# Layer 2 of a four-layer kernel computed in layer 1's order of columns

## The chip, the cores and the metric

The kernel runs on one core of one Trainium2 chip. The metric is the device time of one execution in microseconds (us). A core has TensorE (PE, with its weight loads as PEld), VectorE (DVE), ScalarE (ACT), GpSimd (POOL) and SyncE (SP), each with an instruction stream of its own that runs in order; they wait for each other through semaphores, and DMA queues move data beside them.

## The reference

The input x has the shape (4, 8, 512, 512): 4 images t of 8 channels, rows and columns. Four layers each add to x a layer applied to x normalised in groups (`_gn`: 4 groups of 2 channels, mean and variance over the group's channels, rows and columns).

```python
x = x + _L0_conv_ref(_gn(x), ...)   # spiking attention: four products, heads, a scan over t
x = x + _L1_conv_ref(_gn(x), w)     # 13x13 convolution of each channel by itself, reflected borders
x = x + _L2_conv_ref(_gn(x), weight, bias)
x = x + _L3_conv_ref(_gn(x), weight, bias)

def _L2_conv_ref(x, weight, bias):
    sx = MAX_Q / jnp.max(jnp.abs(x))
    sw = MAX_Q / jnp.max(jnp.abs(weight))
    qx = _quantize(x, sx)           # clip(round(v * scale), -127, 127)
    qw = _quantize(weight, sw)
    out_i32 = conv 3x3 of qx and qw, 8 to 8 channels, zeros as padding
    return out_i32 / (sx * sw) + bias

def _L3_conv_ref(input, weight, bias):
    return conv 3x3 of input and weight, 8 to 8 channels, zeros as padding, + bias
```

The change is in layer 2 and touches neither layer 0 nor layer 1.

## The kernel before, in words

Layers 0 and 1 come first and take the first 2511 us. Layer 1 works on columns in four phases: column 4v + g of a row is held at place 128 g + v (g from 0 to 3, v from 0 to 127; PH is 4, NV is 128, D is 512). It writes its result to DRAM (x2d) in this order, called phase order here. Layer 3 and the output need the columns in their own order.

Layers 2 and 3 share one loop (`layers23`, from L1009). A tile has 128 partitions, which hold two windows of 8 rows by 8 channels (6 rows of results each), and 512 columns. 43 tiles make an image; two tiles are a pair, the last pair of an image has one tile of 64 partitions, so an image has 22 pairs and the loop 88 pairs in all, one a step. In step n:

- `load` (L1053) issues pair n + 5's load of x from x2d on SP's queue, into one of 6 buffers.
- `normalise` (L1077) works on pair n + 2. GpSimd copies each tile of x into a tile u and turns phase order into the own order on the way (L1083: reads 128 columns of one phase in a row, writes every fourth place). ScalarE computes y, u scaled and shifted by the group's statistics and by sx (L1088).
- `quantise` (L1095) works on pair n + 1: VectorE rounds y to whole numbers by adding and subtracting a large constant and writes bf16 into xq (L1100), one of three buffers with two columns of zeros on both sides.
- `layer2` (L1109) works on pair n. For each tile TensorE does three bf16 matmuls, one for each horizontal offset dx of the 3x3 kernel (L1118); the vertical offsets and channels are in the weights. VectorE multiplies the product by inv, adds u and writes x3 (L1125, scalar_tensor_tensor), and for some tiles also sums the result on the way (`accum_out`). x3 is a ring in SBUF that holds layer 3's input. The statistics for layer 3's norm come from ScalarE's sum of squares (L1131) for those tiles, which are all full ones for t = 0 and every second one later, and from VectorE's bn_stats (L1136) for the others.
- `halos` (L1140, issued at L1275) copies the rows that neighbouring windows share, by DMA inside x3; SP issues these copies in the first 22 steps and GpSimd after that.
- `layer3` (L1205) works on the pair 25 steps back. GpSimd writes the two edge columns (L1213), TensorE does 24 fp32 matmuls of 64 by 64 (L1220), ScalarE adds the constant (L1229), SP issues the output DMA (L1236).

When an image's last pair has gone through layer 2, `norm3` (L1165) brings its statistics together in small steps: VectorE L1171 to L1182 and L187 to L196, two small TensorE products (L180, gps from gsum), GpSimd's power (L197), and then VectorE makes layer 3's weights band_t (L1189), a value scaled (L1193) and, after a small product ps_const (L1198), the constant (L1202). Layer 3 of that image can't start before these.

The order of the work on each engine is decided when the kernel is built, by a scheduler that is steered by `issue_after`: normalise and quantise are issued behind the last instructions of layer 2, and layer 2 behind them and behind layer 3. So an instruction that waits holds up all that stands behind it on its engine.

Of the kernel before, what the change touches and what calls it, by code (L numbers as in the profile page):

```python
# [31 lines left out]
F32 = mybir.dt.float32  # L35
BF16 = mybir.dt.bfloat16
F16 = mybir.dt.float16
F32R = mybir.dt.float32r
AF = mybir.ActivationFunctionType
ALU = mybir.AluOpType  # L40
# [3 lines left out]
P = 128  # L44
T, B, N, D, H = 4, 8, 512, 512, 8
# [7 lines left out]
ROUND = 12582912.0  # L53
# [3 lines left out]
PH, NV = 4, D // 4  # L57
# [10 lines left out]
N_PAIRS = (W_ALL + 3) // 4  # L68
# [12 lines left out]
def windows(k):  # L81

    p, j = divmod(k, 2)
    every = [(a, 4 * p + 2 * j + (a ^ j)) for a in range(2)]
    return [(a, q) for a, q in every if q < W_ALL]
# [43 lines left out]
def network(ctx: ExitStack, tc: tile.TileContext, i: dict, out: bass.AP):  # L129
    nc = tc.nc  # L130
# [100 lines left out]
    def pool(name, bufs=1, **where):  # L231
        return tc.tile_pool(name=name, bufs=bufs, reuse_waits="tile", **where)
# [4 lines left out]
    r2 = late.tile([P, T, G], F32, name="r2")  # L237
    most = late.tile([P, G], F32, name="most")
    early = {
        "x": ctx.enter_context(pool("x2", 6, side="right")),  # L240
        "u": ctx.enter_context(pool("u2", 4, side="right")),
        "y": ctx.enter_context(pool("y2", 2, side="right")),
        "o": ctx.enter_context(pool("o3", 10, side="right")),
    }
# [16 lines left out]
    with ExitStack() as s:  # L261
        layers23(
            s, tc, x2d, out, ident, ind, mask2, avg_same, group_steps, m2, r2, most, w23, early, pool
        )
# [628 lines left out]
def weights23(tc, i, pool, scratch, ps_1, ident):  # L893


    nc = tc.nc
# [5 lines left out]
    w = {}  # L902
# [65 lines left out]
    ps = ps_1.tile([P, 2, n_taps], F32, tag="misc", name="ps_outer2")  # L968
# [21 lines left out]
            )  # L990


    w["xq"] = [pool.tile([P, 2, D + 4], BF16, name=f"xq_{j}") for j in range(3)]
    for xq in w["xq"]:
        nc.gpsimd.memset(xq, 0.0)
    w["st3"] = [pool.tile([P, W2_N, 6], F32, name=f"st3_{j}") for j in range(2)]
# [12 lines left out]
def layers23(  # L1009
    s, tc, x2d, out, ident, ind, mask2, avg_same, group_steps, m2, r2, most, w, early, pool  # L1010
):
    nc = tc.nc
# [9 lines left out]
    ps = ps_1.tile([1, P], F32, tag="misc", name="ps_most")  # L1022
# [7 lines left out]
    ps = ps_1.tile([P, 1], F32, tag="misc", name="ps_top")  # L1030
# [6 lines left out]
    for mine, src in ((w["m"], m2), (w["r"], r2)):  # L1037
        own = wpool.tile([P, T, G], F32, tag="own", name="own")
# [7 lines left out]

    x3 = s.enter_context(pool("x3")).tile([P, 2 * RING, D + 2], F32, name="x3")

    def tiles(p):
        return [k for k in (2 * p, 2 * p + 1) if k < W2_N]  # L1050

    def slot(t, p):
        return 2 * ((t * N_PAIRS + p) % RING)  # L1053

    ahead, ready = {}, {}
# [17 lines left out]
    def tiles_apart(t, p, n):  # L1073

        return [slice(j, j + 1) for j in range(n)] if (t, p) == (0, 0) else [slice(0, n)]

    def normalise(t, p):  # L1077
        n, n_p = len(tiles(p)), HALF * len(windows(tiles(p)[-1]))
        x = ahead.pop((t, p))[:n_p, :n, :]
        u = early["u"].tile([P, 2, D], F32, tag="u", name="u2")  # L1080
        y = early["y"].tile([P, 2, D], F32, tag="y", name="y2")
        for j in range(n):
            nc.gpsimd.tensor_copy(  # L1083
                u[:n_p, j, :].rearrange("p (v g) -> p v g", g=PH),
                x[:, j, :].rearrange("p (g v) -> p v g", g=PH),
            )
        for j in tiles_apart(t, p, n):
            op = nc.scalar.activation(  # L1088
                y[:n_p, j, :], u[:n_p, j, :], AF.Identity, bias=w["mr"][:n_p, t : t + 1],
                scale=w["r"][:n_p, t : t + 1],  # L1090
            )
        ready[t, p] = u, y[:n_p, :n, :]
        return op.ins

    def quantise(t, p):  # L1095
        u, y = ready[t, p]
        n_p, n, _ = y.shape
        xq = w["xq"][(t * N_PAIRS + p) % 3]
        for j in tiles_apart(t, p, n):
            op = nc.vector.tensor_scalar(  # L1100
                xq[:n_p, j, 2 : D + 2], y[:, j, :], ROUND, ROUND, op0=ALU.add, op1=ALU.subtract
            )
        ready[t, p] = u, xq
        return op.ins

    def by_sums(t):
        return range(0 if t == 0 else 1, W2_N - 1, 1 if t == 0 else 2)

    def layer2(t, p):  # L1109
        ks = tiles(p)  # L1110
        n_p = HALF * len(windows(ks[-1]))
        u, xq = ready.pop((t, p))
        s0 = slot(t, p)
        st3 = w["st3"][t % 2]
        for j, k in enumerate(ks):
            ps = ps_2.tile([P, D], F32, tag="conv2", name="ps_conv2")
            for dx in range(3):
                mm = nc.tensor.matmul(  # L1118
                    ps[:n_p, :], lhsT=w["band2"][:n_p, j, dx, :n_p],
                    rhs=xq[:n_p, j, dx + 1 : dx + 1 + D], start=dx == 0, stop=dx == 2,  # L1120
                )
            own = x3[:n_p, s0 + j, 1 : D + 1]
            sums = w["sums"][t % 2][:, :, k : k + 1]
            summed = k in by_sums(t)
            done["DVE"] = nc.vector.scalar_tensor_tensor(  # L1125
                own, ps[:n_p, :], w["inv"][:n_p], u[:n_p, j, :], op0=ALU.mult, op1=ALU.add,
                accum_out=sums[:, 0, :] if summed else None,
            ).ins
            if summed:
                square = wpool.tile([P, D], BF16, tag="square", name="square")  # L1130
                done["ACT"] = nc.scalar.activation(  # L1131
                    square, own, AF.Square, bias=w["m"][:, t : t + 1], scale=-1.0,
                    accum_out=sums[:, 1, :],
                ).ins
            else:
                done["DVE"] = nc.vector.bn_stats(st3[:n_p, k, :], own).ins  # L1136
        return mm.ins
# [68 lines left out]
    def layer3(t, p, zero, band, const):  # L1206


        ks = tiles(p)
        s0 = slot(t, p)  # L1210
        n_p = HALF * len(windows(ks[-1]))
# [36 lines left out]
    for n in range(n_all + N_PAIRS + LAG):  # L1248
        if n < n_all:
            for m in range(6) if n == 0 else [n + 5]:  # L1250
                if m < n_all:
                    load(*divmod(m, N_PAIRS))


            with ExitStack() as order:
                for op in done.values():
                    order.enter_context(tc.issue_after(op))
                for m in range(3) if n == 0 else [n + 2]:
                    if m < n_all:
                        first = normalise(*divmod(m, N_PAIRS))  # L1260
                for m in range(2) if n == 0 else [n + 1]:
                    if m < n_all:
                        then = quantise(*divmod(m, N_PAIRS))
            with ExitStack() as order:
                for op in (first, then, *behind):
                    order.enter_context(tc.issue_after(op))
                did = layer2(*divmod(n, N_PAIRS))
        next(norm, None)
        if n_chunk < n <= n_all + 3 and n % n_chunk == 3:
            t, p = divmod(n - 3 - n_chunk, N_PAIRS)  # L1270
# [5 lines left out]
        if n >= N_PAIRS + LAG:  # L1276
            t, p = divmod(n - N_PAIRS - LAG, N_PAIRS)
# [41 lines left out]
```

## Time and profile before

| | us |
|---|---|
| median of 3 runs | 2932.97 (2931.45 to 2935.19) |
| the profiled execution | 2934.12 |
| its span in the profile | 2932.3 |
| layers 0 and 1, until about | 2511 |
| layer 2 of t = 0 alone | 2511 to about 2565 |
| first matmul of layer 3 (L1220) | 2588.2 |
| layers 2 and 3 together, until about | 2860 |
| layer 3 alone, until about | 2924 |

TensorE is busy for 2826.4 us of the span, VectorE for 2210.8, GpSimd for 1036.6, ScalarE for 551.0; the mean granted TensorE clock is 0.989 of full speed.

In the profile, a group of instructions is named by its line in the kernel, engine and operation, then what it writes and reads with the shapes, the count, the busy time and the mean duration of one in ns, and after the bar the time that the engine was idle just before it and what ended most of that. In a timeline, each line has the start in us, the duration in us, the instruction and in brackets the idle time before it with its cause; neighbouring instructions of one kind are drawn together (x2, x6).

### The profile page before, as it was taken

The page shows a single profiled execution, that of the slowest core. Times are in us where ns is not written, and L with a number is a line of the kernel's source. Part 1 is how long each engine was busy: PE and PEld are TensorE (multiplying, and loading weights), DVE is VectorE, ACT ScalarE, POOL GpSimd, SP SyncE. Part 2 cuts the span into 40 slices and gives each one's busy share as a digit, 9 for nine tenths or more (in the row PEclk, how much of TensorE's full clock was granted, in tenths as well). Part 3 has the DMA queues.
Part 4 walks back from the last instruction along what each step waited for, and adds up shares of the span by engine and source line. Part 5 has one row for each costly group of instructions (what it writes and reads, how often), then busy time and mean ns, then how long its engine had stood idle before and what let it go on. Part 6 is the DMA issues. An engine that isn't in the chain of part 4 may idle for free. (4 is left out here: it accounts for less than half of the span.)

```text
span 2932.3 us, 36617 instructions
## 1 busy us (share of the span) xinstructions
PE 2826.4 (96%) x12865; PEld 1302.0 (44%) x12865; DVE 2210.8 (75%) x3916; ACT 551.0 (19%) x860; POOL 1036.6 (35%) x1924
## 2 busy tenths in 40 slices
PE   6899999999999999999999999999999999589999
PEld 3454555554555544455455555455333333223334
DVE  7897788688779778868877886886655556887870
ACT  1300010011010001001000000110111111766664
POOL 3342233343234323323422433332211112676650
PEclk9899999999999999999999999999999999999999
DMA  7333322223222223222222122113878779698865
GB/s 182 100 81 80 73 59 66 72 71 78 64 66 66 73 76 70 59 66 66 73 66 51 45 59 51 52 44 87 224 194 222 207 200 242 145 212 214 221 171 147
DMA packets 323895, 322.10 MB, mean 110 GB/s; under 512 B 21431, under 2 KB 237183, under 8 KB 323599
## 3 DMA queue, kind: packets, MB, share of 16 engines
q1 hardware_dynamic: 261872, 237.39, 33.4%
q0 software_dynamic: 19776, 56.14, 6.0%
q10 hardware_dynamic: 42063, 26.23, 3.2%
q8 instruction: 101, 1.65, 0.3%
q14 instruction: 83, 0.68, 0.1%
HBM read 210.57 MB, written 103.60 MB: 107 GB/s over the span
## 5 line engine op out<-in xcount | busy, mean ns | idle before, releaser
L499 PE MATMUL ps_in<-w_v,xn 128*128 128x512 f32 x1024 | 459.2, 598 | 3.0 <-DVE xn L480 3.0
L499 PE MATMUL ps_in<-w_kq,xn 128*128 128x512 f32 x1024 | 450.1, 592 | 0.0
L815 PE MATMUL ps_conv<-x,bt 112*64 112x512 f32 x2048 | 445.0, 592 | 0.8 <-DVE v_p L467 0.8
L499 PE MATMUL ps_in<-xn,w_kq 128*128 128x512 f32 x1024 | 444.6, 592 | 0.0
L535 PE MATMUL ps_b<-toep,vtok 128*64 128x512 bf16 x3072 | 368.9, 384 | 1.0 <-DVE v_o L550 1.0
L475 POOL TENSOR_TENSOR h_v<-h_v,c_v 128x512 f32<-128x512 f32 x96 | 122.0, 1271 | 683.9 <-DVE h_v L474 658.2
L450 ACT ACTIVATE h_q<-v_q,c_half 128x512 f32<-128x512 f32 x96 | 69.2, 721 | 1473.6 <-DVE v_q L446 950.4
L584 POOL COPY x1s<-x1s 128x2 f32<-128x2 f32 (+1 forms) x1024 | 227.7, 277 | 272.3 <-DVE x1s L573 272.3
L562 PE MATMUL ps_out<-wp,so 128*128 128x512 f32 x1024 | 308.9, 444 | 0.0
L499 PEld LDWEIGHTS ps_in<-xn,w_kq 128*128 128x128 f32 x1024 | 194.3, 190 | 233.0 <-issue 223.2
L499 PEld LDWEIGHTS ps_in<-w_kq,xn 128*128 128x128 f32 x1024 | 194.2, 190 | 219.9 <-issue 204.7
L499 PEld LDWEIGHTS ps_in<-w_v,xn 128*128 128x128 f32 x1024 | 190.9, 191 | 218.4 <-issue 210.1
L815 PEld LDWEIGHTS ps_conv<-x,bt 112*64 112x64 f32 x2048 | 144.9, 135 | 290.2 <-issue 288.1
L1220 PE MATMUL ps_conv<-x,band_t 64*64 64x512 f32 x2040 | 251.4, 609 | 3.1 <-DVE band_t L1189 3.1
L535 PEld LDWEIGHTS <-vtok 128*64 128x64 bf16 x3072 | 176.0, 111 | 155.5 <-issue 7.0
L1083 POOL COPY u<-x 128x512 f32<-128x512 f32 (+1 forms) x172 | 211.7, 1266 | 91.8 <-issue 48.2
L562 PEld LDWEIGHTS ps_out<-wp,so 128*128 128x128 f32 x1024 | 192.6, 188 | 94.4 <-issue 58.1
L573 DVE SCALAR_TENSOR_TENSOR x1s<-v_p,xr 128x256 f32<-128x256 f32 x256 | 188.6, 777 | 13.1 <-DMA x<-x1s 2.3
L837 POOL DMA_DIRECT2D x<-xo x128 | 71.6, 566 | 314.0 <-ACT xo L822 299.7
L475 POOL TENSOR_TENSOR h_k<-h_k,c_k 128x512 f32<-128x512 f32 x96 | 123.3, 1284 | 135.9 <-DVE h_k L474 135.9
L822 ACT ACTIVATE xo<-ps_conv,off 128x512 f32<-128x512 f32 x128 | 87.9, 687 | 430.9 <-PE ps_conv L815 314.8
L1125 DVE SCALAR_TENSOR_TENSOR x<-ps_conv,inv,u 128x512 f32<-128x512 f32 (+1 forms) x172 | 121.3, 745 | 56.3 <-PE ps_conv L1118 29.0
(192 smaller groups left out, 3268.5 us busy)
## 6 DMA issues: line engine op xcount, KB each, us to landing
x<-x SPq DMA_DIRECT2D x64, 917.0 KB
x<-x SPq DMA_DIRECT2D x168, 256.0 KB
x<-x1s POOLq DMA_DIRECT2D x128, 262.0 KB, 2.7
xq<-in_x SPq DMA_DIRECT2D x128, 256.0 KB
xr<-in_x SPq DMA_DIRECT2D x128, 256.0 KB
out<-o SPq DMA_DIRECT2D x164, 192.0 KB
xs<-in_x SPq DMA_DIRECT2D x112, 256.0 KB
x<-xo ACTq DMA_DIRECT2D x128, 128.0 KB
```

Of the source, the lines that this page charges most:

```text
L475: nc.gpsimd.tensor_add(h, h, c_twice[n])
L499: mm = nc.tensor.matmul(ps, lhsT=lhsT, rhs=rhs, start=k == 0, stop=k == NC - 1)
L535: nc.tensor.matmul(pb[two * DH : (two + 1) * DH, :], lhsT=v[:, c, h * DH : (h + 1) * DH], rhs=toep[z][:, h, u : u + N], start=c == 0 and z ...
L562: nc.tensor.matmul(ps, lhsT=so[:, k, c * P : (c + 1) * P], rhs=wpT[z][:, k, :], start=k == 0 and z == 0, stop=k == NC - 1 and z == 1,)
L573: nc.vector.scalar_tensor_tensor(own, v.rearrange("p (g v) -> p g v", g=PH)[:, two, :], 1.0, by_phase[:, two, :], op0=ALU.is_ge, op1=ALU.add,)
L584: nc.gpsimd.tensor_copy(x1[:, f, u : u + n], x1[:, fm, um - n + 1 : um + 1][:, ::-1])
L815: mm = nc.tensor.matmul(ps[q * M1 : (q + 1) * M1, :], lhsT=bt[:, z, :], rhs=xt[:, w0 : w0 + N_PS1, z : z + NV], start=z == 0, stop=z == SH ...
L822: nc.scalar.activation(xo[:, a, :], ps, AF.Identity, bias=off[:, t : t + 1])
L837: engine.dma_start(bass.AP(dst.tensor, dst.offset + (q * n_half * W1_OUT * B + b) * D + f * NV, [[B * D, W1_OUT], [W1_OUT * B * D, n_half] ...
L1083: nc.gpsimd.tensor_copy(u[:n_p, j, :].rearrange("p (v g) -> p v g", g=PH), x[:, j, :].rearrange("p (g v) -> p v g", g=PH),)
L1125: done["DVE"] = nc.vector.scalar_tensor_tensor(own, ps[:n_p, :], w["inv"][:n_p], u[:n_p, j, :], op0=ALU.mult, op1=ALU.add, accum_out=sums[ ...
L1220: mm = nc.tensor.matmul(ps[j][b * HALF : (b + 1) * HALF, :], lhsT=band[half, b, dx, :], rhs=x3[half, s0 + j, dx : dx + D], start=dx == 0, ...
```

## The change

Layer 2 now works in phase order throughout. The tile u and its copies are gone. y is computed from x as loaded, quantise writes the pair into an xq of shape [128, 2, 6, 128]: the four phases in places 1 to 4 of the third dimension, and two outer phases beside them. Column 4v - 1, which phase 0 needs as its left neighbour, is phase 3 moved by one; so two GpSimd copies for a pair (L1101 and L1102 of the changed kernel, [128, 2, 127] bf16 each) fill the outer phases from phases 3 and 0. The three matmuls of a tile then take 4 neighbouring phases, 512 columns in one piece, beginning at phase dx. The product is in phase order. VectorE reads it and x in that order and writes each value to its own column of x3: 128 values at every fourth place, four times. x, which is now read by VectorE as well, has 9 buffers instead of 6.

```diff
-        "x": ctx.enter_context(pool("x2", 6, side="right")),
-        "u": ctx.enter_context(pool("u2", 4, side="right")),
+        "x": ctx.enter_context(pool("x2", 9, side="right")),
...
-    w["xq"] = [pool.tile([P, 2, D + 4], BF16, name=f"xq_{j}") for j in range(3)]
+    w["xq"] = [pool.tile([P, 2, PH + 2, NV], BF16, name=f"xq_{j}") for j in range(3)]
...
+    def by_phase(x):
+        return x.rearrange("p (g v) -> p g v", g=PH)
...
     def normalise(t, p):
         n, n_p = len(tiles(p)), HALF * len(windows(tiles(p)[-1]))
         x = ahead.pop((t, p))[:n_p, :n, :]
-        u = early["u"].tile([P, 2, D], F32, tag="u", name="u2")
         y = early["y"].tile([P, 2, D], F32, tag="y", name="y2")
-        for j in range(n):
-            nc.gpsimd.tensor_copy(
-                u[:n_p, j, :].rearrange("p (v g) -> p v g", g=PH),
-                x[:, j, :].rearrange("p (g v) -> p v g", g=PH),
-            )
         for j in tiles_apart(t, p, n):
             op = nc.scalar.activation(
-                y[:n_p, j, :], u[:n_p, j, :], AF.Identity, bias=w["mr"][:n_p, t : t + 1],
+                y[:n_p, j, :], x[:, j, :], AF.Identity, bias=w["mr"][:n_p, t : t + 1],
                 scale=w["r"][:n_p, t : t + 1],
             )
-        ready[t, p] = u, y[:n_p, :n, :]
+        ready[t, p] = x, y[:n_p, :n, :]
...
     def quantise(t, p):
-        u, y = ready[t, p]
+        x, y = ready[t, p]
         n_p, n, _ = y.shape
-        xq = w["xq"][(t * N_PAIRS + p) % 3]
+        xq = w["xq"][(t * N_PAIRS + p) % 3][:n_p, :n]
         for j in tiles_apart(t, p, n):
             op = nc.vector.tensor_scalar(
-                xq[:n_p, j, 2 : D + 2], y[:, j, :], ROUND, ROUND, op0=ALU.add, op1=ALU.subtract
+                xq[:, j, 1 : PH + 1, :].rearrange("p n g v -> p n (g v)"), y[:, j, :], ROUND, ROUND,
+                op0=ALU.add, op1=ALU.subtract,
             )
-        ready[t, p] = u, xq
+        nc.gpsimd.tensor_copy(xq[:, :, 0, 1:], xq[:, :, PH, : NV - 1])
+        nc.gpsimd.tensor_copy(xq[:, :, PH + 1, : NV - 1], xq[:, :, 1, 1:])
+        ready[t, p] = x, xq
...
                 mm = nc.tensor.matmul(
                     ps[:n_p, :], lhsT=w["band2"][:n_p, j, dx, :n_p],
-                    rhs=xq[:n_p, j, dx + 1 : dx + 1 + D], start=dx == 0, stop=dx == 2,
+                    rhs=xq[:, j, dx : dx + PH, :], start=dx == 0, stop=dx == 2,
                 )
...
             done["DVE"] = nc.vector.scalar_tensor_tensor(
-                own, ps[:n_p, :], w["inv"][:n_p], u[:n_p, j, :], op0=ALU.mult, op1=ALU.add,
+                own.rearrange("p (v g) -> p g v", g=PH), by_phase(ps[:n_p, :]), w["inv"][:n_p],
+                by_phase(x[:, j, :]), op0=ALU.mult, op1=ALU.add,
                 accum_out=sums[:, 0, :] if summed else None,
             ).ins
```

The changed kernel's lines stand up to a few lines off those of the kernel before: its L1097 is quantise, L1119 the matmul of layer 2, L1125 still the result, L1190 band_t, L1221 the matmul of layer 3.

The scheduler's order changes with it: at the second and third change of t, band_t and scaled stand on VectorE ahead of the two results of the new image's pair 3 instead of behind them, and ps_const stands on TensorE between that pair's two tiles instead of among layer 3's first matmuls. On GpSimd the two outer-phase copies of a pair stand in order with the halo DMAs and the edge copies.

## The prediction

> **What bounds the kernel now.** The page first, for the engines' shares and the two groups that the change touches; then the busy times by stage; then the timeline inside each stage, since the shares mix stages with different limits.
>
> ```profile
> PE 2826.4 (96%) x12865; PEld 1302.0 (44%) x12865; DVE 2210.8 (75%) x3916; ACT 551.0 (19%) x860; POOL 1036.6 (35%) x1924
> ...
> L1083 POOL COPY u<-x 128x512 f32<-128x512 f32 (+1 forms) x172 | 211.7, 1266 | 91.8 <-issue 48.2
> ...
> L1125 DVE SCALAR_TENSOR_TENSOR x<-ps_conv,inv,u 128x512 f32<-128x512 f32 (+1 forms) x172 | 121.3, 745 | 56.3 <-PE ps_conv L1118 29.0
> ```
>
> Layers 0 and 1 (to about 2511 us) are untouched. By stage (PE, PEld, DVE, ACT, POOL busy, then PE's granted clock):
>
> ```profile
> 2512.00:2562.00 50.00, 31.32 (x125) 12.18 (x123) 47.55 (x99) 49.43 (x97) 46.32 (x37) 0.97 0.73 150
> 2562.00:2588.00 26.00, 10.42 (x38) 4.27 (x36) 23.22 (x47) 10.70 (x18) 15.01 (x16) 0.74 1.03 177
> 2588.00:2664.00 76.00, 76.00 (x562) 24.77 (x561) 62.23 (x103) 57.78 (x93) 55.82 (x70) 1.00 0.89 239
> 2664.00:2690.00 26.00, 22.27 (x117) 7.29 (x112) 19.58 (x37) 12.96 (x22) 16.21 (x17) 0.87 0.80 188
> ```
>
> Stage A (2512 to 2562) is layer 2 of t=0 alone, and ScalarE, VectorE and GpSimd are all nearly full. Stage B (from 2588) is TensorE without a gap, 4.14 us a step of one pair: nothing that stays off TensorE's path counts there. Between stages, when a t ends, TensorE loses time. One step of stage A in the timeline:
>
> ```profile
> 2532.14 0.08 DVE L1125 DVE_READ_ACCUMULATOR x<-ps_conv,inv,u 128x1 f32 x1
> 2532.19 0.71 ACT L1131 ACTIVATE square<-x,m_own 128x512 bf16<-128x512 f32 x1
> 2532.32 1.11 DVE L1100 TENSOR_SCALAR xq<-y 128x1024 bf16<-128x1024 f32 x1
> ...
> 2533.35 0.74 DVE L1125 SCALAR_TENSOR_TENSOR x<-ps_conv,inv,u 128x512 f32<-128x512 f32 x1
> ...
> 2533.60 1.23 ACT L1088 ACTIVATE y<-u,mr_own,r_own 128x1024 f32<-128x1024 f32 x1
> ...
> 2534.02 0.74 DVE L1125 SCALAR_TENSOR_TENSOR x<-ps_conv,inv,u 128x512 f32<-128x512 f32 x1
> ...
> 2534.86 1.12 DVE L1100 TENSOR_SCALAR xq<-y 128x1024 bf16<-128x1024 f32 x1
> ```
>
> ScalarE runs y, square, square without a gap: 2.54 us a step. VectorE's quantise takes 1.11 here and 0.69 (0.61 until the next starts) where no u copy runs beside it; the two results (L1125) start 0.67 apart. So VectorE's own work is 0.61 + 2 x 0.67 = 1.95 us, 0.59 below ScalarE's. At the first change of t:
>
> ```profile
> 2571.38 0.16 DVE L196 TENSOR_SCALAR grstd_x<-gps_x 128x1 f32<-128x1 f32 x1 [0.47 <-PE gps_x L180]
> 2572.23 7.05 DVE L1189 SCALAR_TENSOR_TENSOR band_t<-band,grstd_x,eye 128x384 f32<-128x384 f32 x1 [0.69 <-POOL grstd_x L197]
> ```
>
> The reader is to see 7.05 us for band_t, an instruction that takes 0.61 at 2683.61: six u copies run on GpSimd from 2572.79 to 2578.86. TensorE waits 8.06 for what follows (ps_const, 2579.41). At the next change of t, TensorE loses twice:
>
> ```profile
> 2668.21 0.38 PE L180 MATMUL gps_x<-gsum_x,avg_same 128*128 128x1 f32 x2 [2.18 <-DVE gsum_x L177]
> 2668.52 4.50 PE L1220 MATMUL ps_conv<-x,band_t 64*64 64x512 f32 x24
> ...
> 2684.36 1.04 PE L1220 MATMUL ps_conv<-x,band_t 64*64 64x512 f32 x2 [1.55 <-DVE band_t L1189]
> ```
>
> The 24 matmuls take 4.50 instead of 2.81, since the granted clock halves after each wait. Each such change costs 8.1 us (two steps of 8.4 instead of 4.14), and there are two of them that matter; that of t=3 is hidden.
>
> [...] The trace agrees (band_t 7.05 against 0.61; quantise 1.11 against 0.69; the result of L1125, with one operand in PSUM, stays at 734 to 754 ns). [...] The trace has the same for reads at a step of four words, and no clear row for writes:
>
> ```profile
> L573 DVE SCALAR_TENSOR_TENSOR x1s<-v_p,xr x256: 606/622/1202, 131.4 to 2055.2; 128x256 f32<-128x256 f32 x128
> L401 DVE SCALAR_TENSOR_TENSOR wp_k<-wp,cols,scale_p x4: 1125/1134/1675, 98.1 to 104.5; 128x512 f32<-128x512 f32 x4
> L1213 POOL COPY x<-zero x88: 178/183/731, 2578.8 to 2874.0; 128x4 f32<-128x4 f32 x84, 64x2 f32<-64x2 f32 x4
> ```
>
> L401 with stepped operands takes 1125, contiguous results of that size (L349) 670; L573 takes 606 for half the elements, about 2 ns each.
>
> **The change, part by part.**
>
> 1. *The 172 u copies go* (211.7 us of GpSimd, off the chain). [...] quantise falls from 1.1 to 1.25 us to about 0.65, hidden in stage A behind ScalarE and in stage B behind TensorE. band_t at the first change falls from 7.05 to about 0.6, on the path: **-6.45**. The new copies of the next pair stand there after quantise, which is itself behind band_t[...].
>
> 2. *176 outer-phase copies come* (two a pair, 254 bf16 elements). By L1213 (183 ns for 4) and the u copy's shortest (1051 for 512), 1.71 ns an element: 0.61 us[...]. I take 0.5, so 1.0 us a pair. They now lie between quantise and the matmuls. In stage A quantise of pair n+1 ends some 2.3 us before VectorE needs that pair's first product, whose matmuls take 0.7: 1.0 fits. In stage B quantise ends a step (4.1) ahead. Exposed: at the start of stage A once, **+1.0**, and in the short run before layer 3 (part 4). If they took 1.0 each, stage A would follow them by about 0.3 us a step (+6). They are queued on GpSimd behind halo DMAs and edge copies (L1275, L1213), some of which wait for landings; matmuls, hence VectorE, would wait behind those (a rival below).
>
> 3. *The result's write is stepped by 16 bytes*, 512 elements, 172 times. Unknown d, added to the 0.67: [...] 0.455 by L401[...]. I take 0.50. Stage A: VectorE's step becomes 0.61 + 2 x 1.17 = 2.95 and it, not ScalarE, is the bound. Between the results of the first and the last whole pair (2513.58 and 2563.18) lie 20 steps, 2.48 on average; 20 x (2.95 - 2.48) = **+9.4**, and **+0.5** for the last half tile, on which the norm waits. ScalarE's slack of 0.47 a step hides nothing of this: squares and norm wait for the results. Below d = 0.27 stage A costs nothing.
>
> 4. *From band_t to layer 3's start* VectorE sets the pace: from the quantise of pair 1 (2580.50) to L1220 (2588.19) 7.69. After: two rounds of two results, statistics 0.69 and quantise 0.61, 3.64 each, then copies 1.0 and matmuls 1.41: 9.7, so **+2.0**.
>
> 5. *Stage B*: VectorE 2 x 1.17 + 0.69 + 0.61 = 3.64 of 4.14. Hidden by TensorE; with less slack than half a microsecond, though.
>
> 6. *The two later changes of t*. The chain to gsum loses the stretch of two quantises (about 1.5 us in 2660 to 2666.5) and gains three slower results (1.5). L1171, L1182 and L189, stretched now to 1.07, 1.07 and 1.13, still stand right behind a quantise[...]. In the new order band_t and scaled stand ahead of the results of pair 3, and ps_const among that pair's matmuls: 1.3 us earlier, against 1.0 for two slower results and up to 1.0 behind the copies. I count **0**, with -5 to +2 for both together.
>
> 7. *Pools*: x has nine buffers for a lead of five, so loads wait for nothing new; the same matmuls, with 512 contiguous columns, and y reading x instead of u cost nothing: ScalarE's 1.23 is for the same elements.
>
> Sum: 1.0 + 9.4 + 0.5 - 6.45 + 2.0 = +6.5 us on the profiled execution's 2934.12 (span 2932.3), so 2940.6; the median of the runs lies 1.15 lower: **2939.5 us**.
>
> **Rivals.**
>
> - *A stepped write is free, or nearly (faster)*. Then stage A keeps 2.54, with +1.0 at its start; band_t gives -6.45, the run to layer 3 nothing; and at each later change gsum comes 1.5 us sooner and band_t before TensorE asks, so that one or both half-clock stretches (1.7 each) go too: about -5 each. Sum -15.5: 2917.5, between 2911 and 2925. For it: no row shows a slow write[...]. It decides below d of about 0.43, where the gains and stage A's loss balance.
> - [...]
> - *GpSimd's queue is late*. A pair's copies stand behind edge copies that wait for halo landings (one wait at L1275 is 12.0 us, GpSimd sits idle 4.81 at 2692). Slack is about 4.2 - 1.0 = 3.2 us, so most fit; some four batches at 1 to 3 us beyond it, with a half clock once or twice, give +4 to +12 more: 2943 to 2951.
> - *Nothing changes, since the u copies were off the path*: true of stages A and B, not of band_t, so no case of its own.
>
> **How the numbers follow.** Forecast 0.58 (own range 2930 to 2948, which covers d from 0.42 to 0.58 and part 6), free write 0.22, dear write 0.10, late queue 0.10. A measurement of this kernel can tell about 0.2%, 5.9 us, from no change. The forecast gives 0.04 faster, 0.24 within, 0.30 slower; free write 0.22 faster; dear write 0.10 slower; late queue 0.03 within, 0.07 slower. Faster 0.26, same 0.27, slower 0.47. The range 2916 to 2953 leaves out a third of the free and most of the dear case.
>
> **What would show it.** L1125's row at about 1.2 us (0.74: free[...]). Stage A's step at 2.95 and ScalarE with gaps there. band_t near 0.6 at the first change of t. The two copies at 0.3 to 0.6 us. Stage B still without gaps, and no wait of L1118 on GpSimd there. Wrong if the step of stage A stays at 2.54, if matmuls wait on GpSimd step by step, or if the later changes of t cost well under or over 8.1 us.

## The result, and the profile after

The changed kernel takes 2921.31 us in the median of 5 runs (2919.56 to 2924.93), against 2932.97 before: a ratio of 0.9961 with a 95% interval of 0.995 to 0.9972, 11.7 us faster. Its profiled execution took 2921.53 us, with a span of 2919.3.

From the page of the changed kernel: the engines' busy times, and the rows of the result and of layer 2's matmuls (which the profile books to L1118).

```profile
PE 2819.7 (97%) x12865; PEld 1301.8 (45%) x12865; DVE 2208.5 (76%) x3916; ACT 551.0 (19%) x860; POOL 888.1 (30%) x1928
...
L1125 DVE SCALAR_TENSOR_TENSOR x<-ps_conv,inv,x 128x512 f32<-128x512 f32 (+1 forms) x172 | 187.4, 1185 | 45.7 <-PE ps_conv L1118 45.6
...
L1118 PE MATMUL ps_conv<-xq,band 128*128 128x512 bf16 (+1 forms) x516 | 132.2, 393 | 30.3 <-POOL xq L1101 30.3
```

The stepped write is slow: 1185 ns on average instead of 745. VectorE's total hardly moved all the same, since its quantise fell from 1196 to 694 ns on average. The busy times by stage (PE, PEld, DVE, ACT, POOL, then PE's granted clock; the last two numbers are the DMA engines' mean share and GB/s):

```profile
2512.00:2562.00 50.00, 29.83 (x114) 11.68 (x114) 47.80 (x93) 48.12 (x90) 14.18 (x38) 0.92 0.66 155
2562.00:2588.00 26.00, 13.65 (x49) 5.68 (x46) 23.01 (x55) 14.86 (x27) 7.45 (x19) 0.74 1.06 170
2588.00:2664.00 76.00, 76.00 (x562) 24.84 (x561) 62.74 (x103) 57.41 (x93) 24.03 (x71) 1.00 0.94 243
2664.00:2690.00 26.00, 25.09 (x163) 8.25 (x162) 22.88 (x44) 17.12 (x28) 10.07 (x38) 1.00 1.00 193
```

Look at the last row: around the second change of t TensorE is busy for 25.09 of 26 us at full clock, where it was 22.27 at 0.87. One step of stage A in the timeline of VectorE and GpSimd:

```profile
2530.85 0.72 DVE L1097 TENSOR_SCALAR xq<-y 128x1024 bf16<-128x1024 f32 x1
...
2531.45 1.17 DVE L1125 SCALAR_TENSOR_TENSOR x<-ps_conv,inv,x 128x512 f32<-128x512 f32 x1
2531.70 0.40 POOL L1101 COPY xq<-xq 128x254 bf16<-128x254 bf16 x1 [1.84 <-DVE xq L1097]
...
2532.44 1.19 DVE L1125 SCALAR_TENSOR_TENSOR x<-ps_conv,inv,x 128x512 f32<-128x512 f32 x1
...
2533.43 0.73 DVE L1097 TENSOR_SCALAR xq<-y 128x1024 bf16<-128x1024 f32 x1
```

One result starts 0.99 after the other, not 0.67: the write costs 0.32, although an instruction's own duration rose by 0.43, because the next one starts before it ends. The step is 0.60 + 2 x 0.99 = 2.58, just over ScalarE's 2.54. The first and the second change of t:

```profile
2577.87 0.62 DVE L1190 SCALAR_TENSOR_TENSOR band_t<-band,grstd_x,eye 128x384 f32<-128x384 f32 x1 [0.69 <-POOL grstd_x L198]
```

```profile
2666.83 0.38 PE L181 MATMUL gps_x<-gsum_x,avg_same 128*128 128x1 f32 x2 [0.66 <-DVE gsum_x L178]
2667.14 2.81 PE L1221 MATMUL ps_conv<-x,band_t 64*64 64x512 f32 x24
...
2679.51 0.28 PE L1199 MATMUL ps_const<-scaled,sum 64*64 64x1 f32 x4
```

band_t takes 0.62 instead of 7.05. The wait for gsum is 0.66 instead of 2.18, the 24 matmuls behind it run at full clock (2.81, not 4.50), and TensorE doesn't wait for band_t or scaled at all.

**Where the time went**, span against span. Layers 0 and 1 ended 1.6 us later in this execution (the first y starts at 2511.64 instead of 2510.02), so each stage is measured from that point. No edit below changes these layers, yet the first y starts anywhere from 2507.4 to 2512.2 in the profiled executions (2515.0 in one run whose added copies begin before it). A difference of a few us between medians can come from there, so the time from the first y to the end of the span is given beside it where it matters: 422.3 us in the kernel before, 407.7 in the changed kernel and 407.9 in a second profile of it.

| stretch | before | after | difference | forecast |
|---|---|---|---|---|
| first y to first result | 3.56 | 3.97 | +0.4 | +1.0 |
| first result to the last whole pair's first (20 steps) | 49.60 | 51.78 | +2.2 | +9.4 |
| from there to band_t | 9.05 | 10.48 | +1.4 | +0.5 |
| band_t | 7.05 | 0.62 | -6.4 | -6.45 |
| end of band_t to layer 3's first matmul | 8.91 | 9.77 | +0.9 | +2.0 |
| layer 3's first matmul to the end | 344.1 | 331.0 | -13.1 | 0 |
| sum | | | -14.6 | +6.5 |

The last stretch is the two later changes of t: their long steps exceed 4.14 us by 8.6 each before (8.41 and 8.43; 8.40 and 8.43), and by 2.0 and 2.1 after (5.18, 4.76 and 4.45; 5.13, 4.76 and 4.58).

### The profile page after: what moved, and what is told of

Read it like the earlier page. It is cut to its first block, busy times and chain, and to the rows that moved or that the text cites. A ratio compares the mean times of both kernels' runs of the same rounds, so it can differ in the third digit from the quotient of the medians.

```text
span 2919.3 us, 36593 instructions
## 1 busy us (share of the span) xinstructions
PE 2819.7 (97%) x12865; PEld 1301.8 (45%) x12865; DVE 2208.5 (76%) x3916; ACT 551.0 (19%) x860; POOL 888.1 (30%) x1928
## 5 line engine op out<-in xcount | busy, mean ns | idle before, releaser
L1221 PE MATMUL ps_conv<-x,band_t 64*64 64x512 f32 x2040 | 242.6, 595 | 0.0
L1125 DVE SCALAR_TENSOR_TENSOR x<-ps_conv,inv,x 128x512 f32<-128x512 f32 (+1 forms) x172 | 187.4, 1185 | 45.7 <-PE ps_conv L1118 45.6
L1118 PE MATMUL ps_conv<-xq,band 128*128 128x512 bf16 (+1 forms) x516 | 132.2, 393 | 30.3 <-POOL xq L1101 30.3
```

What stands on the lines that cost most here:

```text
L1118: mm = nc.tensor.matmul(ps[:n_p, :], lhsT=w["band2"][:n_p, j, dx, :n_p], rhs=xq[:, j, dx : dx + PH, :], start=dx == 0, stop=dx == 2,)
L1125: done["DVE"] = nc.vector.scalar_tensor_tensor(own.rearrange("p (v g) -> p g v", g=PH), by_phase(ps[:n_p, :]), w["inv"][:n_p], by_phase(x[ ...
L1221: mm = nc.tensor.matmul(ps[j][b * HALF : (b + 1) * HALF, :], lhsT=band[half, b, dx, :], rhs=x3[half, s0 + j, dx : dx + D], start=dx == 0, ...
```

## Experiments

### The two halves apart: no u copies, a contiguous write, no outer copies

*The kernel before without its u copies*, the columns left in phase order, with nine buffers of x:

```diff
-        for j in range(n):
-            nc.gpsimd.tensor_copy(
-                u[:n_p, j, :].rearrange("p (v g) -> p v g", g=PH),
-                x[:, j, :].rearrange("p (g v) -> p v g", g=PH),
-            )
...
-                y[:n_p, j, :], u[:n_p, j, :], AF.Identity, bias=w["mr"][:n_p, t : t + 1],
+                y[:n_p, j, :], x[:, j, :], AF.Identity, bias=w["mr"][:n_p, t : t + 1],
...
-        ready[t, p] = u, y[:n_p, :n, :]
+        ready[t, p] = x, y[:n_p, :n, :]
```

The run asks whether the stretched band_t and the losses at the later changes of t go with the u copies.

> The kernel before with the u copies left out: y and the results read x as it was loaded, so the columns stay in layer 1's order and the output is not the reference's; no outer-phase copies, a contiguous write, nine buffers of x. Theory A [...]: stage A stays at ScalarE's 2.54 us a step, band_t about 0.6, no granted clock of 0.5 at the two later changes, each losing at most 1.5 us instead of 8.1; 2912 to 2916 us. Rival B (the losses at the later changes come from the lengths of VectorE's own work[...]): only band_t and some 2 us besides, 2924 to 2927.

2908.9 us (2907.86 to 2910.19), ratio 0.9919 (0.9904 to 0.9934), 23.7 below the kernel before in the same series and lower still than expected. Its waits of TensorE at the second change of t, in the timeline:

```profile
2658.60 0.28 PE L180 MATMUL gps_x<-gsum_x,avg_same 128*128 128x1 f32 x2
2658.81 2.81 PE L1213 MATMUL ps_conv<-x,band_t 64*64 64x512 f32 x24
```

No wait, no half clock: none of its steps around the two later changes is over 4.3 us. So those 8.6 us each, and band_t's 6.4, went with the u copies. In this kernel too band_t stands ahead of pair 3's results, so the new order is part of that; the run with band_t behind the results, below, tells the two apart.

*The changed kernel with the result written contiguously* (layer 3 then works on columns in phase order):

```diff
-                own.rearrange("p (v g) -> p g v", g=PH), by_phase(ps[:n_p, :]), w["inv"][:n_p],
-                by_phase(x[:, j, :]), op0=ALU.mult, op1=ALU.add,
+                own, ps[:n_p, :], w["inv"][:n_p],
+                x[:, j, :], op0=ALU.mult, op1=ALU.add,
```

> The changed kernel with the results written in phase order, contiguously, so that layer 3 sees the columns in the wrong order. Theory A (the stepped write costs 0.32 us an instruction and is hidden by TensorE and almost by ScalarE): results start 0.67 apart, stage A's step 2.54 instead of 2.59, layer 3 starts 2 to 3 us earlier, the later changes of t gain 0 to 0.7 each; 3 to 5 us below the changed kernel. Rival B (the write is what stage A hangs on): 8 us or more.

2917.56 us (2912.18 to 2918.7), ratio 0.9949 (0.9933 to 0.9966): some 3 to 4 below the changed kernel. Its profiled execution was the fastest of its four (2912.18); from the first y to the end it took 401.0, which is 6.7 less. Results start 0.67 apart again, stage A's step is 2.54, and the wait for gsum is gone.

*The changed kernel without outer copies*, the outer phases left at zero:

```diff
-        nc.gpsimd.tensor_copy(xq[:, :, 0, 1:], xq[:, :, PH, : NV - 1])
-        nc.gpsimd.tensor_copy(xq[:, :, PH + 1, : NV - 1], xq[:, :, 1, 1:])
```

> The changed kernel without the two outer-phase copies, so that the outer phases stay zero and two of every four columns' neighbours are partly missing in layer 2; the stepped write and the missing u copies stay. Theory A (the copies are hidden but for the start, the three pairs ahead of layer 3, and a rare late one): 1 to 3 us below the changed kernel; no wait of layer 2's matmuls on GpSimd; the wait for gsum at the later changes falls by 0 to 0.4. Rival B (GpSimd's queue, with its waits for DMA, is a standing cost): 5 us or more below, and less spread between runs.

2916.0 us (2915.17 to 2917.39), ratio 0.9945 (0.993 to 0.996), some 5 below the changed kernel: more than "hidden" allows, at the edge of what the rival expected. From the first y to the end of the span it is 404.9 us against 407.7, so 2.8 in the profiles, which lies in theory A's range; of that about 0.9 lies ahead of layer 3's first matmul, and the rest at the two later changes (long steps 4.71, 4.57 and 4.64, 4.58), where the wait for gsum falls from 0.66 to 0.19. The scheduler's order differs there too, so this isn't the copies' time alone.

The four make a table (medians; the last from two series, 2921.31 and 2920.48):

| without u copies | contiguous write | stepped write |
|---|---|---|
| no outer copies | 2908.9 | 2916.0 |
| outer copies | 2917.6 | 2920.5 to 2921.3 |

By these medians taking the u copies away is worth 23.7, with the new order and the nine buffers that come with it (the buffers were not tested by themselves); the write and the outer copies cost 7.1 and 8.7 alone, and 12 together. The same four from the first y to the end, one profile each and two of the last:

| without u copies | contiguous write | stepped write |
|---|---|---|
| no outer copies | 397.5 | 404.9 |
| outer copies | 401.0 | 407.7 and 407.9 |

There it is 24.8 for the u copies, and 7.4 and 3.5 alone and 10 together for the write and the outer copies: they nearly add. The copies' 8.7 in the medians is thus not shown to be their own.

### The write in the kernel before

The kernel before with u copies kept and the stepped write put in, so that the columns are permuted twice:

```diff
-                own, ps[:n_p, :], w["inv"][:n_p], u[:n_p, j, :], op0=ALU.mult, op1=ALU.add,
+                own.rearrange("p (v g) -> p g v", g=PH),
+                ps[:n_p, :].rearrange("p (g v) -> p g v", g=PH), w["inv"][:n_p],
+                u[:n_p, j, :].rearrange("p (g v) -> p g v", g=PH), op0=ALU.mult, op1=ALU.add,
```

> The kernel before with the stepped write alone: u copies kept, each result written to every fourth column, so that the output's columns are permuted twice. Theory A: VectorE's step in stage A becomes its stretched quantise, 1.1, and two results 0.99 apart, 3.0 to 3.1 instead of 2.54, which is 9 to 11 us; layer 3's start another 1 to 2, each later change of t 0 to 2; 2944 to 2949 us. So the write is cheap in the changed kernel only because the quantise is no longer stretched. Rival B: the write's 0.32 fits beside the copies here too, less than 5 us over the kernel before.

2945.47 us (2945.14 to 2947.36), ratio 1.0045 (1.003 to 1.006). The total is as expected, its parts are not. VectorE in stage A, with GpSimd's u copies of that step:

```profile
2530.29 0.71 DVE L1100 TENSOR_SCALAR xq<-y 128x1024 bf16<-128x1024 f32 x1
...
2530.59 2.44 POOL L1083 COPY u<-x 128x512 f32<-128x512 f32 x2 [0.21 <-ACT square L1133]
2530.90 1.19 DVE L1125 SCALAR_TENSOR_TENSOR x<-ps_conv,inv,u 128x512 f32<-128x512 f32 x1
...
2531.91 1.21 DVE L1125 SCALAR_TENSOR_TENSOR x<-ps_conv,inv,u 128x512 f32<-128x512 f32 x1
...
2532.92 0.72 DVE L1100 TENSOR_SCALAR xq<-y 128x1024 bf16<-128x1024 f32 x1
```

The step is 2.63, not 3.0. In the kernel before the u copies follow each other without a pause (six in 7.72 from 2531.78), and quantise starts while one is running. Here GpSimd waits before each two, they start after quantise has begun, and quantise (0.71) is no longer stretched; the rest of the copies falls beside the results. The rest is lost later, where TensorE waits 3.29 and 3.33 for gsum and 2.17 and 2.18 for band_t (2.18 and 1.55 in the kernel before), and layer 3's start is 5.8 later than before, counted from the first y.

### u copies put back at the later changes

The changed kernel with u copies put back for the pairs around the two later changes alone, into a tile that nothing reads (and eight buffers of x, to make room):

```diff
+    def near(t, p):
+        return t == 1 and p >= 18 or t == 2 and (p <= 5 or p >= 18) or t == 3 and p <= 5
...
+        u = early["u"].tile([P, D], F32, tag="u", name="u2")
+        for j in range(n if near(t, p) else 0):
+            nc.gpsimd.tensor_copy(
+                u[:n_p, :].rearrange("p (v g) -> p v g", g=PH),
+                x[:, j, :].rearrange("p (g v) -> p v g", g=PH),
+            )
```

> The changed kernel, with u copies back on GpSimd for the pairs around the second and third change of t alone (last four of an image, first six of the next), into a tile that nothing reads; eight buffers of x for the room. The order on VectorE and TensorE is that of the changed kernel. Theory A [...]: stage A and the first change as in the changed kernel; quantise, L1172 and L1183's lines stretched again, the wait for gsum back above 1.5 us with a granted clock of 0.5 after it, 3.5 to 7 us at each of the two changes; 7 to 14 us above the changed kernel. Rival B (the new order of instructions alone made the gain): the wait stays at about 0.6 and the time within 2 us of the changed kernel.

2933.82 us (2926.15 to 2937.75), ratio 1.0001 (0.9992 to 1.0009), 12.5 above the changed kernel. The waits for gsum are back, with the order of VectorE's and TensorE's instructions that of the changed kernel:

```profile
2672.08 0.38 PE L181 MATMUL gps_x<-gsum_x,avg_same 128*128 128x1 f32 x2 [2.18 <-DVE gsum_x L178]
...
2770.51 0.38 PE L181 MATMUL gps_x<-gsum_x,avg_same 128*128 128x1 f32 x2 [2.36 <-DVE gsum_x L178]
2770.83 4.49 PE L1231 MATMUL ps_conv<-x,band_t 64*64 64x512 f32 x24
```

So is what makes gsum late, on VectorE, beside a u copy on GpSimd:

```profile
2762.83 0.67 DVE L1107 TENSOR_SCALAR xq<-y 128x1024 bf16<-128x1024 f32 x1
...
2763.19 2.42 POOL L1090 COPY u<-x 128x512 f32<-128x512 f32 x2 [0.73 <-DMA x<-x]
2763.42 1.08 DVE L1182 TENSOR_SCALAR sums<-sums 128x21 f32<-128x21 f32 x1
2764.53 1.21 DVE L1184 COPY st<-sums 128x21 f32<-128x21 f32 x2
```

L1182 and L1184 begin while the copies run and take 1.08 and 1.21; in the changed kernel they take 0.16 and 0.49. Quantise, which had begun before, keeps its 0.67. With the order unchanged, the longer wait is the u copies' work, and the new order alone doesn't account for the gain. But the two changes account for only 4.3 of the 12.5 (long steps 3.5 and 4.8 over, instead of 2.0 and 2.1). Most of the rest is an artefact: u copies ahead of the outer copies wait for x's load, up to 6.07 us, and layer 2's matmuls wait for GpSimd for 10.5 us in all from 2580 on. One such wait has nothing to do with u copies and belongs to the changed kernel's own risk:

```profile
2596.20 0.20 POOL L1224 COPY x<-zero 128x4 f32<-128x4 f32 x1 [4.52 <-DMA x<-x]
...
2598.34 1.46 PE L1128 MATMUL ps_conv<-xq,band 128*128 128x512 bf16 x6 [1.99 <-POOL xq L1111]
```

An edge copy waits 4.52 for a halo's landing, the outer copies stand behind it, and TensorE loses 1.99. The same edge copies wait at this place in every run with outer copies but the run below whose u copies read zeros; TensorE loses 0.49 by it in the second profile of the changed kernel, 0.85 with the contiguous write, and nothing in the first profile.

To be rid of the wait for x the copies were made to read a tile of zeros:

```diff
+    still = wpool.tile([P, D], F32, tag="still", name="still", bufs=1)
+    nc.gpsimd.memset(still, 0.0)
...
-                x[:, j, :].rearrange("p (g v) -> p v g", g=PH),
+                still[:n_p, :].rearrange("p (g v) -> p v g", g=PH),
```

> The run with copies put back around the two later changes of t, but reading a tile of zeros that never changes, so that they wait for no load of x and hold up no outer-phase copy by that[...]. Theory A: the wait for gsum is 1.5 to 2.4 us at each change, with a half clock after it at one of them or both (1.7 each), and hardly a wait of layer 2's matmuls on GpSimd; 3 to 7 us above the changed kernel. Rival B (the rise with the first such copies was their waiting for x alone): within 1.5 us of the changed kernel.

2940.8 us (2938.77 to 2943.96), and no test of the question: with nothing to wait for, the scheduler moved these copies forward, to between 2476 and 2543, so that many of them lie in stage A.

```profile
2527.24 4.84 POOL L1093 COPY u<-still 128x512 f32<-128x512 f32 x4
2532.03 0.39 POOL L1114 COPY xq<-xq 128x254 bf16<-128x254 bf16 x1
```

Four stand between one pair's outer copies and the next's, and three steps of stage A become 5.1 to 6.1 us long. It shows what the outer copies' place on GpSimd means: in stage A they have no slack for other work of that size. At the later changes, where no u copies were left, the waits for gsum are 0.61 and 0.66, as in the changed kernel.

### The order at the later changes

The changed kernel with band_t and scaled behind pair 3's results at those changes:

```diff
-        nc.vector.scalar_tensor_tensor(
-            band, w["band3"], r, w["eye3"], op0=ALU.mult, op1=ALU.add
-        )
...
-        nc.vector.tensor_mul(scaled, zero, r)
-        yield
+        late = t in (1, 2)
+        if late:
+            yield
+            yield
+            yield
...
+        with ExitStack() as behind_results:
+            if late:
+                behind_results.enter_context(tc.issue_after(done["DVE"]))
+            nc.vector.scalar_tensor_tensor(
+                band, w["band3"], r, w["eye3"], op0=ALU.mult, op1=ALU.add
+            )
+            nc.vector.tensor_mul(scaled, zero, r)
+        if not late:
+            yield
```

> The changed kernel with band_t and scaled put behind the results and the statistics of the new image's pair 3 at the second and third change of t, as the kernel before had them behind the results, and ps_const among layer 3's first matmuls again. Theory A (the second loss at each later change is a matter of the order): layer 3's first matmul of the new weights waits 2 to 2.6 us for band_t and may run at half clock after it, 2 to 4 us at each change; 4 to 8 us above the changed kernel. Rival B [...]: the wait stays under 1 us and the time within 2 us of the changed kernel.

2927.45 us (2924.45 to 2931.39), ratio 0.9984 (0.9977 to 0.9992), about 6.5 above the changed kernel.

```profile
2679.09 0.61 PE L1230 MATMUL ps_conv<-x,band_t 64*64 64x512 f32 x1 [2.68 <-DVE scaled L1202]
```

TensorE waits 2.68 and 2.69, and the step is 8.7 instead of 4.45 at both changes. The wait for gsum stays at 0.70 and 0.67. So the second loss at each change is one of order: with no u copies on GpSimd, band_t behind the results still costs it. By the steps in the profile the order is worth 4.3 us a change, 8.5 for both; from the first y to the end it is 8.9, by the medians some 6.5. Of the steps' excess over 4.14 at the two changes together, which is 17.3 us in the kernel before, 12.5 are left with the old order and 4.0 in the changed kernel.

### The length of a wait and the half clock

The changed kernel with additions of zero on gsum's chain:

```diff
+        for _ in range((0, 2, 5, 0)[t]):
+            nc.vector.tensor_scalar_add(st3[:, :, 1], st3[:, :, 1], 0.0)
```

> The changed kernel with additions of zero to the statistics ahead of gsum, on its chain: two at the second change of t, five at the third, about 0.3 us each; the result is the same. Theory A (a wait of TensorE decides the half clock by its length): at the second change the wait for gsum is 1.2 us and the 24 matmuls after it take 2.81, at the third it is about 2 us and they take 4.5. Rival B (length alone doesn't decide, as a wait of 2.18 without a half clock in the run with u copies put back suggests): no half clock at either, or at the shorter one.

2923.61 us (2921.21 to 2925.85). Both as theory A had it:

```profile
2668.70 0.38 PE L181 MATMUL gps_x<-gsum_x,avg_same 128*128 128x1 f32 x2 [1.31 <-DVE gsum_x L178]
2669.01 2.81 PE L1223 MATMUL ps_conv<-x,band_t 64*64 64x512 f32 x24
...
2762.13 0.38 PE L181 MATMUL gps_x<-gsum_x,avg_same 128*128 128x1 f32 x2 [2.03 <-DVE gsum_x L178]
2762.44 4.50 PE L1223 MATMUL ps_conv<-x,band_t 64*64 64x512 f32 x24
```

But length alone isn't the rule. The wait of 2.18 in the run with u copies put back has no half clock behind it (2.81 for the 24 matmuls), while 2.18 and 1.55 in the kernel before have. In the profiles of the kernel before and of the changed kernel all changes of the granted clock in layers 2 and 3 lie on one grid of 3.413 us: in the kernel before, half clock begins at 2668.62, 2685.68 and 2767.61, which are 5 and 24 times 3.413 apart, and in the changed kernel it ends at 2519.71 and begins again at 2570.91, 15 times. So a wait can be placed against such a grid; for the other two runs it is laid on their own half clocks by the same step. Here is the stretch of it that holds the wait, with the next one, for the kernel before, the run with u copies put back and the third change of t in this run (TensorE's busy time, then its granted clock, DMA share and GB/s):

```profile
2665.20:2668.62 3.42, 1.24 (x10) 1.00 0.71 180
2668.62:2672.03 3.41, 3.41 (x20) 0.50 0.98 173
...
2668.47:2671.88 3.41, 1.43 (x6) 1.00 0.65 69
2671.88:2675.30 3.42, 3.22 (x27) 1.00 0.73 163
...
2759.10:2762.51 3.41, 1.38 (x10) 1.00 0.78 178
2762.51:2765.92 3.41, 3.41 (x20) 0.50 1.06 138
```

The wait of the run with u copies put back (2669.90 to 2672.08) lies across the end of a stretch: 1.98 us of it in one and 0.20 in the next. The other two waits lie whole in one stretch. TensorE was busy for 1.24 and 1.38 us of the stretches that half clock followed, and for 1.43 of the one that it didn't follow. So a wait's place on the grid may account for the difference, but these are three stretches and a margin of 0.05 us. The stretch of the kernel before with the wait of 1.55 for band_t (2682.27 to 2685.68: 1.86 busy, half clock after it) doesn't fit that margin, and stays open; two matmuls have 1.04 of the 1.86, and part of that may be waiting. No run moved a wait against the grid by itself, so what decides the half clock was not shown.

### Other ways to put the columns in order

*The step moved to the reads*: the result is written contiguously, in the order of the columns, and the product and x are read 128 places apart.

```diff
-                own.rearrange("p (v g) -> p g v", g=PH), by_phase(ps[:n_p, :]), w["inv"][:n_p],
-                by_phase(x[:, j, :]), op0=ALU.mult, op1=ALU.add,
+                own.rearrange("p (v g) -> p v g", g=PH),
+                ps[:n_p, :].rearrange("p (g v) -> p v g", g=PH), w["inv"][:n_p],
+                x[:, j, :].rearrange("p (g v) -> p v g", g=PH), op0=ALU.mult, op1=ALU.add,
```

> The changed kernel with the step moved from the write to the reads: the result is written contiguously in the own order of columns, and the product in PSUM and x are read 128 places apart from one element to the next. Same result. Theory A [...]: results 1.06 apart in stage A instead of 0.99, its step 2.75, 3 to 6 us above the changed kernel. Rival B (reads far apart cost no more than the stepped write): within 2 us of the changed kernel, or below.

2921.81 us (2917.61 to 2922.08), ratio 0.9961: no difference that the medians tell. In stage A results start 1.03 apart and the step is 2.66, so reads of this kind cost 0.36, a little more than the write, and less than the 0.46 that L401 had suggested. From the first y to the end it takes 409.3, 1.6 more than the changed kernel, all of it ahead of layer 3.

*The inner matmul first*, so that a tile's first product doesn't wait for the outer copies:

```diff
-            for dx in range(3):
+            for dx in (1, 0, 2):
...
-                    start=dx == 0, stop=dx == 2,
+                    start=dx == 1, stop=dx == 2,
```

> The changed kernel with each tile's three matmuls in the order dx = 1, 0, 2: the first needs only what quantise wrote, the other two need the copies. Same result. Theory A (the copies' wait is seen only at the start, ahead of layer 3 and where GpSimd is late): 0.5 to 2.5 us below the changed kernel, VectorE still sets stage A's step. Rival B (what waits is the whole chain, and the order doesn't matter): within 0.5 us.

2919.97 us (2919.91 to 2920.37), ratio 0.9958 (0.9944 to 0.9973). It was run once more in one series with the changed kernel itself:

> The changed kernel once more, beside the two runs that follow, so that they can be compared on one chip: 2919 to 2925 us.

> The kernel with the inner matmul first once more, against the changed kernel in the same series. Theory A: 0.5 to 2.5 us below it. Rival B: no difference that the intervals tell.

2920.48 (2918.74 to 2921.39) for the changed kernel and 2921.95 (2920.47 to 2924.61) with the inner matmul first: no gain that these runs can tell. The start is 0.4 shorter in its profiles, as the first tile no longer waits; but one of VectorE's statistics has moved in the order, and the way from band_t to layer 3's first matmul takes 11.5 us instead of 9.8. So the gain at the start is real and is lost there. Of the versions that compute the reference none is faster than the changed kernel beyond the spread of the runs.

## Why the prediction was wrong

The costs look right in sum, and the gain was not. Forecast costs: 1.0 + 9.4 + 0.5 + 2.0 = 12.9 us. The runs without u copies put what the write and the outer copies cost together at 2920.5 to 2921.3 less 2908.9, about 12, or at 407.7 less 397.5, about 10. That agreement is in part luck. From the first y to layer 3's first matmul, where the forecast had all 12.9, they cost 6.6 (76.6 us against 70.1 without them); the other 3.6 came later, where it had its gains and costs cancel. Forecast gain: 6.45 us. Measured: 23.7, the kernel before against the same without u copies, or 24.8 from the first y.

- *Part 1, the u copies.* band_t was right to a tenth (6.4). That the shorter quantise is "hidden in stage A behind ScalarE and in stage B behind TensorE" was right there. What the sum left out is the later changes of t, where nothing hides a stretched instruction.
- *Part 6, the two later changes: this is the step that failed*, 0 forecast and -13.1 measured. Three things in it were wrong. First, it had L1171, L1182 and L189 stretched after the change as before, since they "still stand right behind a quantise". They take 0.16, 0.28 and 0.26 us. In the kernel before a u copy is running when each of them starts:

```profile
2659.68 2.62 POOL L1083 COPY u<-x 128x512 f32<-128x512 f32 x2 [1.81 <-issue]
2660.08 1.26 DVE L1100 TENSOR_SCALAR xq<-y 128x1024 bf16<-128x1024 f32 x1
2661.26 1.07 DVE L1171 TENSOR_SCALAR sums<-sums 128x21 f32<-128x21 f32 x1
...
2664.42 3.08 POOL L1083 COPY u<-x 128x512 f32<-128x512 f32 x2 [1.59 <-DVE x L1125]
2665.00 1.58 DVE L1100 TENSOR_SCALAR xq<-y 128x1024 bf16<-128x1024 f32 x1
2666.50 1.07 DVE L1182 TENSOR_SCALAR st<-st,b 128x86 f32<-128x86 f32 x1
```

  In the changed kernel the outer copies must wait for quantise, and the next short instruction is done or under way before they start:

```profile
2660.84 0.67 DVE L1097 TENSOR_SCALAR xq<-y 128x1024 bf16<-128x1024 f32 x1
2661.43 0.16 DVE L1172 TENSOR_SCALAR sums<-sums 128x21 f32<-128x21 f32 x1
...
2661.62 0.49 DVE L1174 COPY st<-sums 128x21 f32<-128x21 f32 x2
2662.12 0.41 POOL L1101 COPY xq<-xq 128x254 bf16<-128x254 bf16 x1
2662.15 0.42 DVE L1175 TENSOR_SCALAR sums<-sums,m_own 128x21 f32<-128x21 f32 x1
...
2665.20 0.67 DVE L1097 TENSOR_SCALAR xq<-y 128x1024 bf16<-128x1024 f32 x1
2665.79 0.28 DVE L1183 TENSOR_SCALAR st<-st,b 128x86 f32<-128x86 f32 x1
```

  From the last whole pair's statistics (2660.23; 2659.47 before) to the end of gsum this chain is 6.5 us, and was 8.7. The outer copies, 0.40 long against 1.27 and over in 0.74, still stretch what runs beside them: L1174, L1175, L1176 and L188 take 0.49, 0.42, 0.30 and 0.40 instead of 0.27, 0.28, 0.18 and 0.27 in the run without outer copies, 0.6 in all. Second, the two half clocks of 1.7 each were priced in the rival and left out of the forecast, though the same chain of waits decides both. Third, band_t ahead of the results was set off against slower results and the wait behind the new copies; the run with the old order shows that the order by itself is worth some 6.5 by the medians and 8.5 by the steps. The forecast also took each change's cost before as 8.1, though two steps of 8.4 instead of 4.14 make 8.5.
- *Part 3, the write.* The mechanism was right (VectorE sets stage A's step), the size was not: 0.50 forecast, 0.32 measured. The 0.50 was an estimate, set near the stepped reads of L401 (0.46 for 512 elements). What counts is the spacing of the instructions, 0.99 against 0.67. The 0.32 is 0.63 ns for each of 512 elements. The two prices lie on either side of an edge: ScalarE's pace covers a write of up to 0.27 (half of what VectorE's 1.95 leaves of the step's 2.48 on average), and 0.32 is just above, so it cost 2.2 us in 20 steps and not 9.4. On the norm's path after stage A, part 3's half tile, the loss was 1.4 instead of 0.5, as the last pair's results stand on it too.
- *Parts 2 and 4.* The copies take 0.40, not the 0.5 of the estimate, and show where part 2 said: at the start (+0.4) and ahead of layer 3 (+0.9 instead of +2.0). They were not wholly hidden elsewhere: leaving them out gives some 5 us by the medians and 2.8 from the first y, most of the latter at the later changes.
- *Part 5.* Stage B stayed TensorE's, without a gap in the profiled execution.
- *The rivals.* The free write had the later changes right, -5 each against -6.5 measured, and named both reasons, an earlier gsum and band_t before TensorE asks; its price for the write was wrong. These are separate questions that the forecast had tied together. Its total of 2917.5 lies close to the measured 2921.3, in part by luck: too small a gain at the later changes made up for a write that it had at nothing. The late queue is real but small: up to 1.99 us at one halo landing, 0.49 and nothing in the two profiles of the changed kernel. A dear write, one that costs more than the forecast's 0.50, is excluded by the 0.32.

## What to carry to other kernels

A helper engine's work that is off the path still has a price where it stretches the work of the path's engine: band_t took 7.05 us beside six u copies and 0.62 without them. Look for it in the stage that nothing covers, here the few short instructions between two long stages, and compare each one's duration there with its usual one (L1171: 1.07, and 0.16 in the changed kernel). When two effects meet in a chain of waits, price each by itself before setting one off against the other; and where a waiting TensorE runs at half clock afterwards, that belongs to the wait's price: here 4.50 us instead of 2.81 for 24 matmuls. For an instruction that stands in a row of its kind, take the spacing of the starts (0.99 for the stepped result) and not the duration (1.17).

## What was not expected of the hardware

- A stepped write has a tail that overlaps the next instruction: durations of 1.17 to 1.19 us at a spacing of 0.99; later in stage A durations reach 1.48 (2563.46) at a spacing still close to 1.0.
- By the spacing of starts, 512 elements cost VectorE 0.46 us more with reads at steps of four words (L401, 1.05 against 0.59 for the contiguous L349, one pair of starts), 0.32 more with such writes, and 0.36 more with reads 128 words apart, one of the two operands in PSUM (1.03 against 0.67).
- Two waits of TensorE of the same length, 2.18 us, were followed by half clock in one kernel and by full clock in another, where the wait lay across a point of the 3.413 us grid.
- In the lines shown, the stretching of VectorE depends on which began first: a quantise that began before the u copies took 0.71 and 0.67, one that began beside a running copy 1.11 and 1.26. band_t took 7.05 beside a row of six u copies, and 0.62 without them.
